# Four layers on one core: sums of denominators by matmul, scores moved, a bias multiplied as a row

## The chip, the cores and the metric

The kernel runs on one core of a Trainium2 chip. The metric is the device time of one execution in microseconds (us). Before the change it was 3402.58 us, the median of three runs (3399.19 to 3405.2).

## The reference

The input x has two images of 512 channels and 1024 pixels (32 by 32), all in float32. Four layers follow each other: layer 0 is a deformable attention with a learned bias and an MLP, layers 1 to 3 are attentions over the pixels of each image. Layer 1 has eight heads, layers 2 and 3 have one. The parts that the change touches are these:

```python
# layer 1: the projection and its bias; v carries the bias qkv_b[1024:]
out = jnp.einsum('oc,bcl->bol', proj_w, hh) + proj_b[None, :, None]
# layer 2
attn = jax.nn.softmax(jnp.einsum('bci,bcj->bij', q, k) * scale, axis=-1)
out = jnp.einsum('bcj,bij->bci', v, attn)
x = x + jnp.einsum('bchw,oc->bohw', out, w_proj) + b_proj
# layer 3: 64 channels in q and k
q = jnp.einsum('dc,bcn->bdn', wq, f) + bq[:, None]
k = jnp.einsum('dc,bcn->bdn', wk, f) + bk[:, None]
v = jnp.einsum('dc,bcn->bdn', wv, f) + bv[:, None]
qk = jnp.einsum('bdi,bdj->bij', q, k)
attn = jax.nn.softmax(qk, axis=1)
o = jnp.einsum('bci,bij->bcj', v, attn)
return gamma * o.reshape(b, c, h, w) + x
```

Layer 3's softmax is over the first pixel index, the one that is summed over with v.

## The kernel before

Layer 0 fills the first 2450 us or so and is not touched. Layers 1 to 3 (and layer 0's MLP) are in the function `layers`, from line 1053 on. An order is written out by hand there: inside `in_order` every engine takes its instructions in the order in which the program issues them, so an instruction that waits holds up everything behind it on its engine.

Large products are done in blocks of two by two with seven products in place of eight (a Strassen-like scheme). The function `group` (line 1370) does one such product: it takes four PSUM banks x, y, v and z out of eight that rotate, and calls `add(out, l, r)` seven times; each call is a run of `nk` matmuls with left block number `l` and right block number `r`. Copies on ScalarE (ACT) and sums on VectorE (DVE), called p1, p5, u2 (line 1413) and u3 (line 1424), prepare what `evict` then writes. Some of the seven operands on each side are sums of blocks (on the left s4 at number 2, s1 at 4, s2 at 5; on the right t4 at 3, t1 at 4, t2 at 5), made by `left_sums` (lines 1356 to 1359) and `right_sums` (lines 1365 to 1368).

The sums, normalizations and divisions that are not part of a group are "chores". They stand in queues (`Track`), and `do_chores(us, budget)`, which `group` calls three times, moves a planner's clock on by `us` and issues chores from the queues, in the order of the list `tracks`, until their planned costs use up `budget`. A number in a queue is a wait in the planner's clock. `flush` issues all that is left. The planner's clock only decides the place in the program; it is not the time on the chip.

In layers 2 and 3 each image is handled in two halves of 512 pixels. For each half there is an object of the class `Weights`: u0 and u1 in layer 2; in layer 3, a0 and a1 for image 0, b0 and b1 for image 1. `grow` makes the scores and their exponentials, in four chunks p. Each chunk holds two blocks of 128 pixels by 512. Where `shares` is true (layer 3), the weights themselves are multiplied by the reciprocals (`normalize`, line 1853, 128 by 1024 each) before they are used; in layer 2 the result is (line 1888). The denominators come about like this:

```python
if c % 2 and self.shares or c == 1:
    self.acc.append(unit("acc"))
    self.add(self.acc[-1], p[c - 1], p[c])   # DVE, line 1813
...
self.track.extend((2.0, (0.1, self.total), 4.0, (0.4, self.divisor)))
if self.shares:
    self.track.append(5.0)
```

`total` (line 1834) multiplies the sums by ones, on four column tiles of 32, copies the result to SBUF and sends it over DMA into the layout 128 by 4 (`few`); `divisor` (lines 1844 to 1849) adds the four parts, inverts them, and sends them to DRAM (`d`) and from there to all partitions (`r`).

The value groups (`values`, called by `layer_values`) make v transposed, named vT, with products named pmv; vs are the left sums of them. `weighed` multiplies v by the weights, in two groups per half (products named pw), and adds the result to x. In layer 3 it then stores x. SyncE (SP) issues all these DMAs on one queue.

Layer 3 before went: scores of a0; second weighting of layer 2's image 1; value groups of image 0, with two `grow` of a1 after the first and two after the second; weighting of a0 with the projections of image 1 between its groups; scores of b0; weighting of a1; value groups of image 1 with the scores of b1 among them; weighting of b0; weighting of b1.

In layer 1, `projection_bias` (line 1702) multiplies the bias of v by the projection: sixteen products with one column each, into the bank pb. p_b is used in `add_projection`, in products named ppr.

Of the kernel before, what the change touches and what calls it, by code (L numbers as in the profile page):

```python
# [12 lines left out]
F32 = mybir.dt.float32  # L13
# [6 lines left out]
P = 128  # L20
# [60 lines left out]
def kernel(ctx: ExitStack, tc: tile.TileContext, a: dict, out: bass.AP):  # L81
# [971 lines left out]
    def layers(f, fold_d, t2_b, o2_b):  # L1053
# [330 lines left out]
        def group(name, nk, n, stationary, moving, evict, slack, plain=False):  # L1384

            third = nk * n / 256

            x, y, v, z = [bank(name)[:, :n] for _ in range(4)]

            def add(out, l, r, start=True):  # L1390
                for k in range(nk):
                    nc.tensor.matmul(  # L1392
                        out,
                        stationary(l, k),
                        moving(r, k),
                        start=start and k == 0,
                        stop=k == nk - 1,
                        skip_group_check=not start,
                    )

            if plain:
                for out, (l, r) in ((x, (0, 0)), (y, (6, 0)), (v, (0, 6)), (z, (6, 6))):
                    add(out, l, r)
                    add(out, 1 if l == 0 else 3, 1 if r == 0 else 2, False)
                evict((x, None), (v, None), (y, None), (z, None))
                return
            later, put_off[:] = list(put_off), []
            add(x, 0, 0)
            p1 = temp("p1", n)
            nc.scalar.copy(p1, x)  # L1410
            add(y, 5, 5)
            u2 = temp("u2", n)
            nc.vector.tensor_tensor(u2, y, p1, ALU.add)  # L1413
            add(v, 4, 4)
            p5 = temp("p5", n)
            nc.scalar.copy(p5, v)
            at_once(later)
            do_chores(third, slack)
            add(z, 3, 3)
            add(x, 1, 1, False)  # L1420
            do_chores(third, slack)
            add(y, 6, 6, False)
            u3 = temp("u3", n)
            nc.vector.tensor_tensor(u3, y, p1, ALU.add)
            add(v, 2, 2, False)
            evict((x, None), (v, u2), (z, u3), (p5, u3))
            do_chores(third, slack)
# [78 lines left out]

        def values(seven_w, seven_h, s, vt):

            vq = vt.rearrange("p (k m n) -> p k m n", k=2, m=2)

            def evict(c11, c12, c21, c22):
                put(vq[:, 0, 0], c11)
                put(vq[:, 0, 1], c21)
                put(vq[:, 1, 1], c22)
                put(vq[:, 1, 0], c12)

            group(
                "pmv", 2, QUARTER,
                lambda i, k: seven_h[i][:, k, s * P : (s + 1) * P], lambda i, k: seven_w[i][:, k, :], evict, 1.1,
            )  # L1520
# [178 lines left out]
        p_b = keep.tile([P, CC], F32, name="p_b")  # L1699

        def projection_bias():
            pb = bank("pb")
            for m in range(CC):
                accumulate(
                    pb[:, m : m + 1],
                    [(proj1[k // 2][:, k % 2, m * P : (m + 1) * P], vb[:, 0, k : k + 1]) for k in range(CC)],
                )
            nc.vector.tensor_tensor(p_b, pb[:, :CC], col("proj_b", 0, CC), ALU.add)

# [7 lines left out]
        to_w = track()  # L1717
        to_w.append((0.3, projection_bias))
        w_p = weights_p()
        in_time(to_w, 0.5, left_sums(*w_p))  # L1720
        qs, ks = heads(seven_h)
        vt = every_value(seven_v, seven_h)
        flush(to_w, to_o)
        add_projection(xs[0], seven_left(*w_p), seven_o)
# [48 lines left out]

        def layer_values(seven_w, seven_h):

# [7 lines left out]
            def steps():  # L1783
                for s in range(4):
                    vt.append(unit("vT"))
                    values(seven_w, seven_h, s, vt[s])
                    unformed.append(s)
                    if s == 2:
                        sv.extend(unit("vs") for _ in range(3))
                    while sv and unformed:  # L1790
                        in_time(t_s, 0.45, left_sums(*parts(unformed.pop(0))))
                    yield
# [3 lines left out]
        class Weights:  # L1796

            def __init__(self, score, order, at, shares):
                self.score, self.order, self.at, self.shares = score, order, at, shares
                self.p, self.acc, self.spare, self.track = [], [], None, track()  # L1800

# [13 lines left out]
            def grown(self, c):  # L1815
                p = self.p
                if c % 2 and self.shares or c == 1:
                    self.acc.append(unit("acc"))
                    self.add(self.acc[-1], p[c - 1], p[c])
                elif c > 1 and not self.shares:  # L1820
                    self.add(self.acc[0], self.acc[0], p[c])
                if not self.shares:
                    for i in ((), (0, 1), (2,), (3,))[c]:
                        self.form(i)
# [3 lines left out]
            def total(self):  # L1828
                den, row = bank("den"), temp("row", HALF)
                n = 2 * len(self.acc)  # L1830
                self.few = small.tile([P, 4, HALF // P], F32, name="few2")
                for i in range(n):
                    acc = self.acc[i // 2].rearrange(self.order, k=2, q=2)
                    nc.tensor.matmul(den[32 * i : 32 * i + 32], ones[:, :32], acc[:, i % 2], start=True, stop=True)
                nc.scalar.copy(row[: 32 * n], den[: 32 * n])
# [5 lines left out]
            def divisor(self):  # L1841
                few = self.few[:, 0]
                for i in range(1, 2 * len(self.acc)):
                    nc.vector.tensor_add(few, few, self.few[:, i])
# [3 lines left out]
                nc.sync.dma_start(out=d.rearrange("(q n) -> q n", q=P), in_=few)  # L1848
                nc.sync.dma_start(out=self.r, in_=d.partition_broadcast(P))

            def normalize(self, c):
# [15 lines left out]
            def finish(self):  # L1867
                self.track.extend((2.0, (0.1, self.total), 4.0, (0.4, self.divisor)))
                if self.shares:
                    self.track.append(5.0)  # L1870
                    for c in range(4):
                        self.track.append((1.2, lambda c=c: self.normalize(c)))
                        self.form(c)

        def weighed(name, x, qb, seven_sv, w, bias, done=None):

            n = slice(qb * HALF, (qb + 1) * HALF)
            for g in range(2):

                def evict(c11, c12, c21, c22):  # L1880
# [15 lines left out]

                group(name, 4, QUARTER, lambda i, s: seven_sv(i, s)[:, g * P : (g + 1) * P], w.seven, evict, 2.6)
                yield
# [24 lines left out]
        for b in range(B):  # L1923
# [21 lines left out]
            if b == 0:  # L1945
                flush(to_h)
                to_h = track()
                seven_h = normed(to_h, norm, h2s[1], "h2")
                flush(u0.track, to_v)
                drain(weighed("pw2", xs[0], 0, value2, u0, o2_b))  # L1950
                flush(u1.track)
                drain(weighed("pw2", xs[0], 1, value2, u1, o2_b))
# [37 lines left out]

        def scores3(qb, both):

# [3 lines left out]
            def score(c):  # L1996
                p = unit("p3")
                for part, (l, r) in enumerate(((qk, kq), (kq, qk))):
# [31 lines left out]

        flush(u0.track, to_v)
        seven_x, to_x = pixels3(xs[0])
# [8 lines left out]
        for c in range(4):  # L2041
            a0.grow(c)
        flush(u1.track)
        drain(weighed("pw2", xs[1], 1, value2, u1, o2_b))
        flush(to_x)
        value3, value_steps, to_v = layer_values(seven_v3, seven_x)
        for c in range(2):
            advance(value_steps)
            a1.grow(2 * c)
            a1.grow(2 * c + 1)  # L2050
        drain(value_steps)
        flush(a0.track, to_v)
        steps = weighed("pw3", xs[0], 0, value3, a0, gb3, store(0))
# [3 lines left out]
        drain(steps)  # L2057
        b0, b1 = [scores3(qb, both) for qb in range(2)]
        for c in range(4):
            b0.grow(c)  # L2060
        flush(a1.track)
        drain(weighed("pw3", xs[0], 1, value3, a1, gb3, store(0)))
        flush(to_x)
        value3, value_steps, to_v = layer_values(seven_v3, seven_x)
        for c in range(2):
            advance(value_steps)
            b1.grow(2 * c)
            b1.grow(2 * c + 1)
        drain(value_steps)
        flush(b0.track, to_v)  # L2070
        steps = weighed("pw3", xs[1], 0, value3, b0, gb3, store(1))
        advance(steps)
        checks = guard()
        drain(steps)
        flush(b1.track)
        advance(checks)
        steps = weighed("pw3", xs[1], 1, value3, b1, gb3, store(1))
        advance(steps)
# [101 lines left out]
```

## The time and profile before

| What | us |
|---|---|
| median of three runs | 3402.58 |
| the profiled execution | 3400.25 |
| its span, first to last instruction | 3398.4 |
| PE busy in the span | 3351.9 |
| PE busy from 3350 to 3398 us (48 us) | 34.57 |
| four den products in layer 3 (eight records) | 1.00 |
| one normalize step on DVE (128 by 1024) | 1.22 |
| r<-d, from issue to landing, median from 3150 us on | 4.2 |
| few<-row, the same | 2.0 |
| out<-x, the same | 2.1 |

PE is TensorE's matmuls, PEld its weight loads, DVE VectorE, ACT ScalarE, SP SyncE's DMA queue. A float32 matmul leaves two records in the trace, so "x8" are four matmuls. The clock that the profile gives for PE is the share of full speed that was granted.

### The profile page before, as it was taken

How to read it: one execution, taken by the hardware profiler on the slowest of the kernel's cores; microseconds unless marked ns; L12 is line 12 of the kernel's file. 1: busy time of each engine (PE TensorE's matmuls, PEld its weight loads, DVE VectorE, ACT ScalarE, POOL GpSimd, SP SyncE). 2: the span in 40 equal slices, each digit the busy share in tenths (PEclk: the TensorE clock that was granted, in tenths of full speed). 3: DMA queues.
4: the chain of work that ended last, by engine and by line, in shares of the span. 5: the costliest groups of instructions: out<-in, count | busy, mean ns of one | idle time of the engine just before them, and what ended most of it. 6: DMA issues, size and time to landing. Idle time of an engine off the chain costs nothing.

```text
span 3398.4 us, 61331 instructions
## 1 busy us (share of the span) xinstructions
PE 3351.9 (99%) x24853; PEld 1615.5 (48%) x24853; DVE 2662.6 (78%) x3461; ACT 1803.4 (53%) x2764; POOL 464.0 (14%) x563
## 2 busy tenths in 40 slices
PE   9999999999999999999999999999999999999998
PEld 4333332333333333333333338999953533678676
DVE  6999999999997899999998954455456465756565
ACT  4866867867866667867867641112136245212221
POOL 0222222222221122222222210000000000000000
PEclk9999999999999999999999999999999999999999
DMA  5676676676775576676776641000100010000110
GB/s 167 149 151 139 141 153 143 139 153 138 148 149 118 110 150 138 149 148 137 150 147 142 141 124 57 14 11 11 51 0 14 26 35 14 7 7 5 28 38 30
DMA packets 146707, 320.31 MB, mean 94 GB/s; under 512 B 31088, under 2 KB 76784, under 8 KB 145648
## 3 DMA queue, kind: packets, MB, share of 16 engines
q0 software_dynamic: 56880, 199.79, 30.9%
q1 hardware_dynamic: 88240, 111.80, 10.9%
q8 instruction: 198, 3.24, 0.4%
q10 hardware_dynamic: 1296, 4.72, 0.4%
q14 instruction: 93, 0.76, 0.1%
HBM read 71.46 MB, written 10.83 MB: 24 GB/s over the span
## 4 chain that ended last, share of the span: by engine, by line
PE 77%; DVE 16%; issue 4%; ACT 2%; DMA 1%; ACTq 0%; POOL 0%; DVEq 0%; SPq 0%; POOLq 0%
PE z L543 35%; DVE wa L526 6%; PE pma L136 5%; PE pw L1392 5%; PE pmb L136 4%; DVE h L557 4%; PE pmv L1392 4%; PE score L1568 3%; PE pv L1580 3%; PE pm L1392 3%; PE score L1392 3%; DVE h L526 2%; PE pmp L136 2%; PE pp L629 2%; PE ppr L1392 1%
## 5 line engine op out<-in xcount | busy, mean ns | idle before, releaser
L543 PE MATMUL z<-wa,cpb_w 128*32 128x512 f32 x11904 | 1779.1, 593 | 6.7 <-DVE simbias L490 3.4
L552 ACT ACTIVATE h<-z,b2h 128x1024 f32<-128x1024 f32 x1024 | 1134.2, 1114 | 529.6 <-PE z L543 506.2
L543 PE MATMUL z<-h,cpb_w 128*32 128x512 f32 x4480 | 986.3, 593 | 3.3 <-ACT h L552 2.2
L543 PEld LDWEIGHTS z<-wa,cpb_w 128*32 128x32 f32 x11904 | 492.9, 110 | 883.6 <-issue 804.6
L526 DVE CUSTOM_DVE_ANT_1 wa<-tab,tab 128x1024 f32<-128x1024 f32 x744 | 878.2, 1216 | 34.0 <-PE z L543 33.9
L557 DVE SCALAR_TENSOR_TENSOR h<-h,turn,h 128x1024 f32<-128x1024 f32 x512 | 653.3, 1276 | 8.8 <-ACT h L552 8.6
L543 PEld LDWEIGHTS z<-h,cpb_w 128*32 128x32 f32 x4480 | 256.2, 110 | 335.0 <-issue 291.8
L832 POOL DMA_DIRECT2D h<-h x255 | 227.9, 894 | 1055.0 <-DVE h L557 711.4
L526 DVE CUSTOM_DVE_ANT_1 h<-tab,tab 128x1024 f32<-128x1024 f32 x280 | 332.9, 1216 | 10.5 <-PE z L543 10.4
L1214 ACT COPY p<-pma 128x128 f32<-128x128 f32 x70 | 18.6, 266 | 305.6 <-PE pma L136 305.6
L1569 ACT ACTIVATE p<-score 128x512 f32<-128x512 f32 x256 | 130.0, 626 | 81.2 <-PE score L1568 80.4
L1206 DVE TENSOR_TENSOR upper<-pma,p 128x256 f32<-128x256 f32 x70 | 29.5, 421 | 163.6 <-ACT p L1214 163.5
L825 POOL DMA_DIRECT2D h<-h x126 | 110.9, 880 | 322.4 <-DMA h<-h 319.0
L829 POOL DMA_DIRECT2D h<-h x126 | 119.0, 944 | 155.2 <-DMA h<-h 148.8
L1601 DVE TENSOR_TENSOR acc<-acc,p 128x1024 f32<-128x1024 f32 x96 | 111.1, 1217 | 20.7 <-ACT p L1569 20.6
L1568 PE MATMUL score<-q,k 64*128 64x512 f32 x512 | 120.7, 604 | 1.1 <-DVE gm L1088 1.1
L1580 PE MATMUL pv<-p,vT 128*64 128x512 f32 x512 | 116.5, 598 | 0.0
L1392 PE MATMUL pw<-p,vT 128*128 128x256 f32 x384 | 91.5, 385 | 6.9 <-DVE p L1853 6.9
L513 ACT ACTIVATE tab<-tab,pc 128x512 f32<-128x512 f32 x126 | 96.2, 763 | 0.0
L1392 PE MATMUL pmv<-wa,hc 128*128 128x256 f32 x384 | 89.7, 380 | 5.2 <-DVE u L1413 5.2
L347 ACT ACTIVATE products<-qpad,pc 128x64 f32<-128x64 f32 x252 | 85.5, 407 | 0.0
L1392 PEld LDWEIGHTS pw<-p,vT 128*128 128x128 f32 x384 | 72.4, 191 | 24.2 <-DVE p L1853 8.4
(432 smaller groups left out, 3680.2 us busy)
## 6 DMA issues: line engine op xcount, KB each, us to landing
h<-h POOLq DMA_DIRECT2D x255, 512.0 KB, 5.0
h<-h POOLq DMA_DIRECT2D x252, 256.0 KB, 4.7
tab<-slog_d SPq DMA_DIRECT2D x128, 256.0 KB, 4.6
h<-h SPq DMA_DIRECT2D x126, 256.0 KB, 2.3
r<-d SPq DMA_DIRECT2D x24, 256.0 KB, 3.5
xt<-in_xt SPq DMA_DIRECT2D x8, 512.0 KB, 7.6
wa<-in_mlp_w SPq DMA_DIRECT2D x4, 1024.0 KB, 7.9
wb<-in_mlp_w SPq DMA_DIRECT2D x16, 256.0 KB, 5.6
```

The source lines that it names most:

```text
L136: nc.tensor.matmul(pm, w, m, start=(k == 0), stop=(k == len(pairs) - 1))
L526: nc.vector._custom_dve(TENSOR_ADD_SAT, out=h1.rearrange("p (y x) -> p y x", x=W), in0=tx[:, quad, point, :].unsqueeze(1).to_broadcast([P, ...
L543: nc.tensor.matmul(z[point * 32 : point * 32 + 32, n], cpb_w2[:, lo : lo + 32], h1s[point][:, n], start=True, stop=True,)
L552: nc.scalar.activation(h2, z, AF.Relu, bias=b2h[:, part : part + 1])
L557: nc.vector.scalar_tensor_tensor(h2, h2, turn[:, part // 2 : part // 2 + 1], parts.pop(part + 1), ALU.mult, ALU.add)
L829: nc.gpsimd.dma_start(out=joins[i - 3][1:P:2], in_=joins.pop(i - 2)[1:P:2], accum_op=ALU.add)
L832: nc.gpsimd.dma_start(out=joins[i - 1], in_=other, accum_op=ALU.add)
L1392: nc.tensor.matmul(out, stationary(l, k), moving(r, k), start=start and k == 0, stop=k == nk - 1, skip_group_check=not start,)
L1568: nc.tensor.matmul(sc, ks[m][r, s * P : (s + 1) * P], qs[m][r, n], start=True, stop=True)
L1569: nc.scalar.activation(p[:, part], sc, AF.Exp, scale=64 ** -0.5)
L1580: nc.tensor.matmul(pv[half][part * 64 : part * 64 + 64], vt[s % 4][:, lo : lo + 64], lps[s, half][:, part, :], start=(s == 0), stop=(s == 7),)
L1601: nc.vector.tensor_add(acc[half], acc[half], ps[s, half])
```

## The change

- `group` with more than two chunks (`nk` > 2: the weightings of layers 2 and 3) calls `add(z, 3, 3)` second, right after `add(x, 0, 0)`, not fourth.
- `projection_bias` is split. `bias_row` takes the bias as the stationary operand, 32 columns wide by repetition, and the projection as the moving one, in four products on four column tiles; a copy and four small DMAs bring the row into 128 by 4 by 4. The four parts are added on DVE later.
- In layer 3 the denominators are products of ones with all four p, accumulated in PSUM; the sums acc on DVE go away.
- `total` and `divisor` of layer 3 stand in a queue of their own, `chain`, at the head of the list of queues; the planner's waits around them are 6.5, not 4.0 and 5.0. For layer 2 the first is 6.5 as well, in its old queue.
- a1's scores are grown ahead of the first two value groups, not after them. The value groups of layer 3 may do more chores in each third (1.7, not 1.1).
- b1's scores are made between and after the two groups of the weighting of a1, a weighting and more earlier; they lie in unused columns of the weights tile w_3.
- The last group of all evicts straight into x, in quarters of 256 columns.

```diff
@@ group
             nc.scalar.copy(p1, x)
+            if nk > 2:
+                add(z, 3, 3)
             add(y, 5, 5)
...
             do_chores(third, slack)
-            add(z, 3, 3)
+            if nk == 2:
+                add(z, 3, 3)
             add(x, 1, 1, False)
@@ layer 1
+        def bias_row():
+            pb, row = bank("pb"), temp("row", HALF)
+            for k in range(CC):
+                nc.tensor.matmul(
+                    pb[32 * k : 32 * k + 32],
+                    vb[:, 0, k : k + 1].to_broadcast([P, 32]),
+                    proj1[k // 2][:, k % 2, :].rearrange("p (m q) -> p q m", m=CC),
+                    start=True,
+                    stop=True,
+                )
+            nc.scalar.copy(row, pb)
+            with nc.allow_non_contiguous_dma("2048 numbers"):
+                for k in range(CC):
+                    nc.sync.dma_start(
+                        out=p_few[:, k], in_=row[32 * k : 32 * k + 1].rearrange("o (q m) -> o q m", m=CC)
+                    )
+
         def projection_bias():
-            pb = bank("pb")
-            for m in range(CC):
-                accumulate(
-                    pb[:, m : m + 1],
-                    [(proj1[k // 2][:, k % 2, m * P : (m + 1) * P], vb[:, 0, k : k + 1]) for k in range(CC)],
-                )
-            nc.vector.tensor_tensor(p_b, pb[:, :CC], col("proj_b", 0, CC), ALU.add)
+            nc.vector.tensor_tensor(p_b, p_few[:, 0], col("proj_b", 0, CC), ALU.add)
+            for k in range(1, CC):
+                nc.vector.tensor_add(p_b, p_b, p_few[:, k])
...
-        to_w.append((0.3, projection_bias))
+        to_w.append((0.3, bias_row))
+        to_b = track()
+        to_b.extend((15.0, (0.5, projection_bias)))
@@ Weights
-                if c % 2 and self.shares or c == 1:
-                    self.acc.append(unit("acc"))
-                    self.add(self.acc[-1], p[c - 1], p[c])
...
                 den, row = bank("den"), temp("row", HALF)
-                n = 2 * len(self.acc)
+                some = [p.rearrange(self.order, k=2, q=2) for p in (self.p if self.shares else self.acc)]
+                n = self.n = min(4, 2 * len(some))
...
+                for i in range(2 * len(some)):
+                    j = i % n
+                    nc.tensor.matmul(
+                        den[32 * j : 32 * j + 32],
+                        ones[:, :32],
+                        some[i // 2][:, i % 2],
+                        start=i < n,
+                        stop=i + n >= 2 * len(some),
+                    )
...
                 nc.sync.dma_start(out=self.r, in_=d.partition_broadcast(P))
+                if self.shares:
+                    self.track.ready = clock[0] + 6.5
+                    for c in range(4):
+                        self.track.append((1.2, lambda c=c: self.normalize(c)))
+                        self.form(c)
...
-                self.track.extend((2.0, (0.1, self.total), 4.0, (0.4, self.divisor)))
-                if self.shares:
-                    self.track.append(5.0)
...
+                (self.chain if self.shares else self.track).extend((2.0, (0.1, self.total), 6.5, (0.4, self.divisor)))
@@ weighed
+                def evict_last(c11, c12, c21, c22):
+                    for (base, more), i, q in ((c11, 0, 0), (c21, 1, 0), (c22, 1, 1), (c12, 0, 1)):
+                        m, at = g + 2 * i, qb * HALF + q * QUARTER
+                        dst = x[:, m, at : at + QUARTER]
+                        if more is not None:
+                            nc.vector.tensor_add(dst, dst, more)
+                        nc.vector.scalar_tensor_tensor(dst, base, bias[:, m : m + 1], dst, ALU.add, ALU.add)
+                        if q:
+                            done(m, n)
@@ scores3
-                p = unit("p3")
+                p = unit("p3") if places is None else places[:, c * HW : (c + 1) * HW]
@@ layer 3
-        value3, value_steps, to_v = layer_values(seven_v3, seven_x)
+        value3, value_steps, to_v = layer_values(seven_v3, seven_x, 1.7)
         for c in range(2):
-            advance(value_steps)
             a1.grow(2 * c)
             a1.grow(2 * c + 1)
+            advance(value_steps)
...
-        b0, b1 = [scores3(qb, both) for qb in range(2)]
+        spare = HALF + CC * C + 6 * QUARTER
+        b0, b1 = [scores3(qb, both, places) for qb, places in ((0, None), (1, w_3[:, spare : spare + CC * HW]))]
...
-        drain(weighed("pw3", xs[0], 1, value3, a1, gb3, store(0)))
-        flush(to_x)
-        value3, value_steps, to_v = layer_values(seven_v3, seven_x)
-        for c in range(2):
-            advance(value_steps)
+        for c, _ in enumerate(weighed("pw3", xs[0], 1, value3, a1, gb3, store(0))):
             b1.grow(2 * c)
             b1.grow(2 * c + 1)
+        flush(to_x)
+        value3, value_steps, to_v = layer_values(seven_v3, seven_x, 1.7)
...
-        steps = weighed("pw3", xs[1], 1, value3, b1, gb3, store(1))
+        steps = weighed("pw3", xs[1], 1, value3, b1, gb3, store(1), True)
```

## The prediction

> **What bounds the kernel now.** I read the page first, then TensorE's waits, then the timeline and the granted clock around the longest of them. Nothing before 2640 us changes in the order of any engine's work, so the question is what the last 760 us hold.
>
> ```profile
> PE 3351.9 (99%) x24853; PEld 1615.5 (48%) x24853; DVE 2662.6 (78%) x3461; ACT 1803.4 (53%) x2764; POOL 464.0 (14%) x563
> ```
>
> PE is busy 99% of the span, so a gain must come out of PE's own work, out of its few waits, or out of the end. The waits of PE from 2640 us on (engine, line, whom for, us in total, times, longest):
>
> ```profile
> PE pw L1392 <- DVE p L1853: 6.9, 3, 3.1
> PE pmv L1392 <- DVE u L1413: 5.2, 3, 3.7
> PE pw L1392 <- DVE vs L1357: 3.5, 4, 0.9
> PE score L1568 <- DVE gm L1088: 1.1, 1, 1.1
> PE score L1392 <- DVE u L1413: 0.7, 1, 0.7
> ```
>
> Only 17.4 us. But two of them cost more than they last. The timeline of PE, then the busy time and granted clock of stretches behind the two (PEclk is the number before the last two):
>
> ```profile
> 3212.41 1.13 PE L1392 MATMUL pmv<-wa,hc 128*128 128x256 f32 x4 [3.71 <-DVE u L1413]
> ...
> 3333.63 2.43 PE L1392 MATMUL pw<-pt,vs 128*128 128x256 f32 x10 [0.88 <-DVE vs L1357]
> ...
> 3359.76 0.70 PE L1392 MATMUL pw<-p,vT 128*128 128x256 f32 x2 [3.09 <-DVE p L1853]
> 3362.61 1.22 PE L1392 MATMUL pw<-p,vT 128*128 128x256 f32 x2 [2.15 <-DVE p L1853]
> 3365.45 1.22 PE L1392 MATMUL pw<-p,vT 128*128 128x256 f32 x2 [1.63 <-DVE p L1853]
> 3366.47 5.65 PE L1392 MATMUL pw<-pt,vs 128*128 128x256 f32 x16
> ```
>
> ```profile
> 3214.00:3216.00 2.00, 2.00 (x5) 0.84 (x5) 1.93 (x6) 0.00 (x0) 0.00 (x0) 0.50 0.00 0
> ...
> 3368.00:3370.00 2.00, 2.00 (x6) 1.55 (x6) 0.28 (x2) 0.00 (x0) 0.00 (x0) 0.50 0.00 0
> ```
>
> The reader is to see that after each pause the matmuls run at half the clock: sixteen records that take 3.62 us elsewhere took 5.65. Who keeps DVE from serving PE stands in DVE's timeline:
>
> ```profile
> 3202.00 1.22 DVE L1853 TENSOR_TENSOR p<-p,r 128x1024 f32<-128x1024 f32 x1 [5.21 <-DMA r<-d]
> ...
> 3352.66 1.23 DVE L1853 TENSOR_TENSOR p<-p,r 128x1024 f32<-128x1024 f32 x1 [4.51 <-DMA r<-d]
> ```
>
> DVE takes its instructions in order, and waits for the broadcast of the reciprocals with evictions queued behind it. Last, two pieces of the chain of waits that price PE's own work (start, us, what):
>
> ```profile
> 2648.84 3.47 PE pb L136 x32
> ...
> 3187.66 1.00 PE den L1834 x8
> ```
>
> [...] Here one-column pb records last 250 ns, their weight loads 192 ns. [...]matmuls on different column tiles overlap; four den products (eight records of about 605 ns) take 1.00 us together. [...]no strided moving operand is in the part of the trace I looked at, so its price is open.
>
> **The change, part by part.**
>
> *A. Last weighting (weights b1).* Before, b1 is scored between the value groups; den runs at 3339.5, r lands at 3352.6, and each of the four normalize steps with its sums takes about 2.9 us of DVE (1.22 and four of 0.42), so the fourth chunk is ready at 3365.4 where PE wanted it at 3357.4. That group runs from 3356.08 to 3378.95, 22.87 us; the next, of the same 56 records, takes 12.2 (3379.07 to 3391.28). Excess: 10.7 us, of which 6.9 are waits and 3.8 clock. After, b1's scores stand inside the weighting of a1, den in the first value group, and its normalize steps inside the two groups of b0. From den to b1's use lie over three value groups (6.05 each) and two weighting groups (12.2 each), 43 us. The chain wants 0.6 (row), 2.6 (four issues at 0.65), 2.0 (landing), 0.6, 1.6 (d), 4.2 (r) and 11.7 (four steps): 23 us. The planner adds waits of its own, yet some 5 to 20 us stay over. −10.7. What is late next there: nothing; the vs sums of value group four were needed earlier.
>
> *B. Wait of 3.71 us in image 0's value groups.* Before, a0's first normalize stands ahead of u3 of the last pw2 group and waits 5.21 us for r, so evictions slip, then two more normalize steps go ahead of the value groups' u. The matmuls from 3212.41 to 3217.90 take 5.5 us where their records at full clock take 3.65: 1.85 on top, 5.55 in all. After, the divisor is set 6.5 units behind the sums and normalize another 6.5 behind it, one unit being about a microsecond (a third of a weighting group counts 4 and lasts 4.1), against 5.6 to 5.8 us measured from divisor to r. The new order has the first normalize behind the eviction of the last pw2 group, with no DMA wait. Laid out by hand from the end of that group's matmuls: its eviction takes DVE to 3.4, normalize and sums to 6.3, u2, second normalize and sums to 9.7, half of a third (1.2) to 10.9, u3 to 11.3. PE does four scores (1.92), a value group (to 8.0), four scores (to 9.9); the next value group wants its y bank at 10.8, which is free at 11.3. So about 0.6 us of wait stay[...]. −4.95; bounds −5.5 and 0 (a wait of the old size).
>
> *C. The four vs waits.* With four chunks, add(z,3,3) now comes second. Its operands are a plain block of vT and a sum of weights formed long before; it gives DVE 1.73 us more ahead of the first vs product, and each wait was 0.87. All four go: −3.5. z's bank is wanted earlier, but eight banks rotate and its last reader is a group or four scores back.
>
> *D. Value bias as a row.* 16 products of one column (3.47 us) become four of 32 rows by 512 columns on four column tiles. At den's price 1.0[...]. I take 1.5: −2.0 (bounds −2.5 and +0.5). The ACT copy (0.58), four small DMAs on SP's queue (2.6 us of issue, ahead of a division's few), and four small adds on DVE lie beside heads and value groups; p_b is wanted by ppr 60 us later. Nothing on the path; up to 1 us if SP's d and r behind them slip.
>
> *E. Denominators from the weights.* Eight adds of 1.22 us leave DVE (9.8 us, not on the path as such), and four weightings get four more den products each: 4 × 1.0 = +4.0, fully on PE. Bounds +3.0 and +6 (if accumulating on a tile just used keeps them from overlapping).
>
> *F. End.* Before, the last x ends 2.1 us after the last matmul (c 0.44, x 0.67, x 0.74). After, u3 and seven 256-wide operations (0.42 each, 0.34 to 0.46 apart) start at the same point, 1.5 us before the last matmul ends, and end about 1.7 behind it: −0.4. Stores land in 2.1 us as before.
>
> *G. Value groups with slack 1.7, scores moved ahead, layer 2's later divisor.* DVE's load in image 0's value groups: 4 × 2.1 of evictions, 11.7 of normalize, 7.2 of vs sums, 27 us against PE's 24.2 + 3.8 + 2.0 = 30. It fits, less tightly than before without the adds. 0.
>
> Sum: −10.7 −4.95 −3.5 −2.0 +4.0 −0.4 = −17.5. The profiled execution took 3400.25 (span 3398.4 and 1.9 around it), 2.3 below the median of 3402.58. That gives 3382.7 from the one and 3385.1 from the other; I take 3384.
>
> **Rivals.**
> 1. DVE is late again in the value groups (27 of 30 us leaves little): waits [...]bring the half clock, at B's old price of 5.5 per image: 3384 + 5.5 to 11, about 3392. For it: u3 stands behind up to 4 us of queued sums. Against it: the layout above gives 0.6, and image 1 has no scores there any more.
> 2. D and E cost their upper bounds, +2.5 and +2: 3388.5.
> 3. Slower: the broadcast r, on SP's one queue with 256 KB stores, lands later than the planner's 6.5 units, and each weighting stalls as b1's did (10.7). To end above 3409 it takes 25 us back, so three of four weightings: 3384 + 32 = 3416. It decides where divisor to r passes about 9 us instead of 5.8. Against it: in SP's new order stores stand between the sums and the broadcast of b0 alone.
> 4. The change doesn't do what it says, b1's normalize steps staying late because the weights in w_3's spare columns make scores wait for readers of w_3: A is lost, 3395. The last such readers are long done.
>
> **How the numbers follow.** Main case 0.78, its own range 3379 to 3389. Rival 1 0.09, rival 2 0.07, rival 3 0.03, rival 4 0.03. The low end is every bound on the good side (D −2.5, E +3, B −5.5, and one microsecond at the end): about −20.5 to −23, 3378. The high end takes in rival 1: 3393. Differences under 0.2% (6.8 us) can't be told from none here. Faster is the main case, rivals 1 and 2 nearly whole, and half of 4: 0.93; same 0.04; slower 0.03.
>
> **What would show it.** Right: no wait of pw for the normalize line, no clock below 1 behind 3150 us, the last weighting's two groups alike at about 12.2 us, no wait for vs, den rows of about 2 us for x16, pb of 1 to 2 us, one pmv wait of some 0.6 in image 0. Wrong: DVE waiting for r with u3 behind it, a pmv wait over 3 us, or den rows well above 2 us.

## The result, and the profile after

| | before | after |
|---|---|---|
| median of six runs (lowest to highest), us | 3402.41 (3399.19 to 3405.2) | 3380.89 (3380.24 to 3382.41) |
| profiled execution, us | 3400.25 | 3381.55 |
| its span, us | 3398.4 | 3379.8 |

The ratio after to before is 0.9939, with a 95% interval of 0.9929 to 0.9949. The change took off 21.5 us by the medians and 18.6 us between the two profiled spans. The work ahead of 2644 us, where nothing changes, ran 0.66 us longer in the profiled execution of after (the first pm behind the last pv starts at 2644.16, before at 2643.50), so behind it 19.3 us went. The terms below are measured against that. The profiled execution of before was one of its faster ones (3400.25 us against a median of 3402.41); part D of the account below shows what the slower ones most likely have on top.

The first part of the page after (busy us, share of the span, instructions of each engine), and TensorE's waits from 2640 us on (line waited for, us in total, times, longest):

```profile
PE 3348.8 (99%) x24861; PEld 1611.8 (48%) x24861; DVE 2654.9 (79%) x3458; ACT 1804.6 (53%) x2764; POOL 464.7 (14%) x563
```

```profile
PE score L1571 <- DVE gm L1088: 1.1, 1, 1.1
PE score L1392 <- DVE u L1415: 0.7, 1, 0.7
PE pmv L1392 <- DVE u L1415: 0.3, 1, 0.3
```

Of 17.4 us of waits 2.1 are left. The waits for the normalize line, for vs and the 3.71 us are gone; the two for scores were there before, and the 0.3 us is what is left of two short waits in layer 2's value groups. PE's busy time fell by only 3.1 us although the half clock is gone as well, because the longer den products give some of it back.

The timeline of TensorE through the last weighting of after, and the busy time and granted clock (third from the end) of the stretch that ran at half clock before:

```profile
3347.73 1.89 PE L1392 MATMUL pw<-wa,vT 128*128 128x256 f32 x8
...
3358.09 1.89 PE L1392 MATMUL pw<-wa,vs 128*128 128x256 f32 x8
...
3360.03 1.99 PE L1392 MATMUL pw<-wa,vT 128*128 128x256 f32 x8
...
3370.49 1.89 PE L1392 MATMUL pw<-wa,vs 128*128 128x256 f32 x8
```

```profile
3368.00:3370.00 2.00, 2.00 (x11) 1.77 (x10) 0.00 (x0) 0.00 (x0) 0.00 (x0) 1.00 0.05 12
```

The two groups of that weighting now take 12.25 and 12.35 us from first to last matmul, at full clock: the first lost 10.6 of its 22.9 us, and the weighting as a whole 10.7 (35.35 to 24.65).

The chain of waits of after (start, us, what) prices the pieces of PE's own work that the change touched:

```profile
2649.51 2.26 PE pb L1709 x7
...
2991.16 12.09 PE pw L1392 x56
3003.25 0.98 PE den L1855 x4
3004.23 36.46 PE pw L1392 x168
...
3183.45 1.85 PE den L1855 x16
```

The reader is to see three things. The bias row costs 2.26 us, against 3.47 for the sixteen single columns. Eight den products (sixteen records) cost 1.85 us, against 1.00 for four. And the weighting of layer 2's image 0 runs from 2991.16 without a pause: with its den it takes 49.53 us to 3040.69. Before, the timeline has for the same records, and for the first ones behind them:

```profile
2992.92 1.89 PE L1392 MATMUL pw<-p,vT 128*128 128x256 f32 x8
...
3043.59 1.88 PE L1392 MATMUL pmt<-hc,wa 128*128 128x512 f32 x4
```

That is 50.67 us, with one wait of about 0.9 for vs in them, so that wait cost 1.14.

Last, DVE's timeline at the end of after:

```profile
3370.69 0.42 DVE L1427 TENSOR_TENSOR u<-pw,p 128x256 f32<-128x256 f32 x1 [4.68 <-PE pw L1392]
3371.04 0.47 DVE L1916 SCALAR_TENSOR_TENSOR x<-pw,gb,x 128x256 f32<-128x256 f32 x1
...
3373.72 0.48 DVE L1916 SCALAR_TENSOR_TENSOR x<-pw,gb,x 128x256 f32<-128x256 f32 x1
```

The last matmul ends at 3372.38, DVE at 3374.20. From the last matmul to the end of the span there are 7.4 us, against 7.0 before: the new end is not shorter.

### The profile page after: what moved, and what is told of

Read it like the earlier page. It is cut to its first block, busy times and chain, and to the rows that moved or that the text cites. A ratio compares the mean times of both kernels' runs of the same rounds, so it can differ in the third digit from the quotient of the medians.

```text
span 3379.8 us, 61349 instructions
## 1 busy us (share of the span) xinstructions
PE 3348.8 (99%) x24861; PEld 1611.8 (48%) x24861; DVE 2654.9 (79%) x3458; ACT 1804.6 (53%) x2764; POOL 464.7 (14%) x563
## 4 chain that ended last, share of the span: by engine, by line
PE 79%; DVE 15%; issue 4%; ACT 2%; DMA 0%; POOL 0%; DVEq 0%; SPq 0%; ACTq 0%; POOLq 0%
PE z L543 35%; DVE wa L526 6%; PE pw L1392 6%; PE pma L136 5%; PE pmb L136 4%; DVE h L557 4%; PE pmv L1392 4%; PE score L1571 3%; PE pv L1583 3%; PE pm L1392 3%; PE score L1392 3%; DVE h L526 2%; PE pmp L136 2%; PE pp L629 2%; PE pmt L1392 1%
## 5 line engine op out<-in xcount | busy, mean ns | idle before, releaser
L1214 ACT COPY p<-pma 128x128 f32<-128x128 f32 x70 | 18.6, 266 | 305.5 <-PE pma L136 305.5
L1571 PEld LDWEIGHTS score<-q,k 64*128 64x128 f32 x512 | 47.3, 186 | 70.3 <-issue 54.9
L1392 PEld LDWEIGHTS pmv<-wa,hc 128*128 128x128 f32 x384 | 72.6, 190 | 14.2 <-issue 2.8
```

The source lines that it names most:

```text
L1392: nc.tensor.matmul(out, stationary(l, k), moving(r, k), start=start and k == 0, stop=k == nk - 1, skip_group_check=not start,)
L1571: nc.tensor.matmul(sc, ks[m][r, s * P : (s + 1) * P], qs[m][r, n], start=True, stop=True)
```

## The experiments

Eight kernels were run. Each was timed against the kernel before on the same chip, whose medians there were 3402.54 us (e1 to e4) and 3403.07 us (e5 to e8). All compute the whole output.

The prediction had the right size for its largest step, A. The question was whether its reason holds. Theory 1 is the prediction's: the stall in the last weighting goes because b1's scores stand a weighting earlier, inside that of a1. Theory 2: b1's scores were early enough before; what came late was what DVE owes to them, the sums acc and the total, which stood behind other chores in b1's queue. The queue of its own at the head of the list, or taking the sums off DVE, cures that wherever the scores are.

### e1: the change with b1's scores back between the value groups

```diff
-        for c, _ in enumerate(weighed("pw3", xs[0], 1, value3, a1, gb3, store(0))):
-            b1.grow(2 * c)
-            b1.grow(2 * c + 1)
+        drain(weighed("pw3", xs[0], 1, value3, a1, gb3, store(0)))
         flush(to_x)
         value3, value_steps, to_v = layer_values(seven_v3, seven_x, 1.7)
+        for c in range(2):
+            b1.grow(2 * c)
+            b1.grow(2 * c + 1)
+            advance(value_steps)
         drain(value_steps)
...
-        b0, b1 = [scores3(qb, both, places) for qb, places in ((0, None), (1, w_3[:, spare : spare + CC * HW]))]
+        b0, b1 = [scores3(qb, both) for qb in range(2)]
```

> The changed kernel, but b1's scores are made ahead of image 1's first two value groups (as a1's are for image 0) and lie in the arena; everything else stays. Theory 1 (the prediction's step A: the early place of the scores is what removes the last stall): a good part of the stall comes back, the first group of the last weighting lasts 17 to 23 us and the median is 3386 to 3391. Theory 2 (the queue of their own is what brings the sums, the inversion and the normalize steps forward; the place of the scores matters little): that group lasts 12.2 us and the median is 3381 as with the change.

Measured: 3382.57 us (3381.55 to 3382.85), ratio 0.9944 (0.9928 to 0.9961), which can't be told from the change's own. The last den in its timeline of PE:

```profile
3308.92 1.92 PE L1855 MATMUL den<-p,ones 128*32 128x512 f32 x16
```

It stands 40 us ahead of the last weighting (3348.87), where the change has 46 (3301.74 to 3347.73). No wait of pw appears. With the queue and the products in place, the early place of the scores is not needed.

### e2: the kernel before with b1's scores early, alone

```diff
-        b0, b1 = [scores3(qb, both) for qb in range(2)]
+        spare = HALF + CC * C + 6 * QUARTER
+        b0, b1 = [scores3(qb, both, places) for qb, places in ((0, None), (1, w_3[:, spare : spare + CC * HW]))]
...
-        drain(weighed("pw3", xs[0], 1, value3, a1, gb3, store(0)))
-        flush(to_x)
-        value3, value_steps, to_v = layer_values(seven_v3, seven_x)
-        for c in range(2):
-            advance(value_steps)
+        for c, _ in enumerate(weighed("pw3", xs[0], 1, value3, a1, gb3, store(0))):
             b1.grow(2 * c)
             b1.grow(2 * c + 1)
+        flush(to_x)
+        value3, value_steps, to_v = layer_values(seven_v3, seven_x)
```

> The kernel before with this alone: b1's scores inside the weighting of a1, in the spare columns of w_3. Theory 1: the last stall goes, -10.7, 3392. Theory 2: b1's sums and inversion still stand behind the chores of b0 and the vs sums in the list of queues, so den stays just ahead of the last weighting and nothing is gained: 3402, last group 22 to 23 us.

Measured: 3402.71 us (3399.74 to 3405.05), ratio 1.0001 (0.9993 to 1.001). Nothing is gained. TensorE's timeline, b1's den and the waits behind it:

```profile
3342.26 1.06 PE L1834 MATMUL den<-acc,ones 128*32 128x512 f32 x8
...
3362.24 1.22 PE L1392 MATMUL pw<-wa,vT 128*128 128x256 f32 x2 [2.74 <-DVE wa L1853]
3365.08 1.22 PE L1392 MATMUL pw<-wa,vT 128*128 128x256 f32 x2 [1.63 <-DVE wa L1853]
3367.93 1.22 PE L1392 MATMUL pw<-wa,vT 128*128 128x256 f32 x2 [1.63 <-DVE wa L1853]
```

And DVE's timeline, the sums over b1's weights among b0's normalize steps, and the sums for vs behind them:

```profile
3296.89 1.21 DVE L1813 TENSOR_TENSOR acc<-wa 128x1024 f32<-128x1024 f32 x1
3310.56 1.21 DVE L1853 TENSOR_TENSOR p<-p,r 128x1024 f32<-128x1024 f32 x1
...
3323.03 1.22 DVE L1853 TENSOR_TENSOR p<-p,r 128x1024 f32<-128x1024 f32 x1
3327.49 1.22 DVE L1813 TENSOR_TENSOR acc<-wa 128x1024 f32<-128x1024 f32 x1
3328.96 0.41 DVE L1356 TENSOR_TENSOR vs<-vT 128x256 f32<-128x256 f32 x1
...
3336.78 0.42 DVE L1359 TENSOR_TENSOR vT<-vT 128x256 f32<-128x256 f32 x1
```

b1's last scores end at 3308.2, 9 us earlier than before by the same view. But the second sum comes at 3327.49, behind all four normalize steps of b0. Then the sixteen sums for vs follow (3328.96 to 3337.20), and only then total: the den at 3342.26 is 16.6 us ahead of the last weighting (3358.90), the same as before (3339.44 to 3356.08). The early scores only wait longer. Theory 1 falls.

### e3: the kernel before with the queue of its own, alone

The sums stay on DVE, and move into the queue too. The planner's waits are 6.5, as in the change.

```diff
-self.p, self.acc, self.spare, self.track = [], [], None, track()
+self.p, self.acc, self.spare, self.chain, self.track = [], [], None, track(True), track()
...
-                self.track.append((1.2, lambda: nc.vector.tensor_add(acc, one, other)))
+                (self.chain if self.shares else self.track).append((1.2, lambda: nc.vector.tensor_add(acc, one, other)))
...
-                self.track.extend((2.0, (0.1, self.total), 4.0, (0.4, self.divisor)))
-                if self.shares:
-                    self.track.append(5.0)
+                (self.chain if self.shares else self.track).extend((2.0, (0.1, self.total), 6.5, (0.4, self.divisor)))
```

> The kernel before with this alone: layer 3's sums (still on DVE), total and divisor in a queue at the head of the list, the planner's waits 6.5. Theory 1: the last stall stays as it was, 22.9 us; only part of the 3.7 us wait goes, 3398 or so. Theory 2: the last stall shrinks to one wait of about 2 us without the half clock (-8), and the 3.7 us wait to about 2.4 (-3): 3391.

Measured: 3393.6 us (3389.62 to 3395.48), ratio 0.9975 (0.9966 to 0.9984), 9 us faster (5.4 to 11.6 by the interval). TensorE's timeline:

```profile
3215.30 2.07 PE L1392 MATMUL pmv<-wa,hc 128*128 128x256 f32 x4 [2.16 <-DVE u L1413]
...
3327.72 1.06 PE L1834 MATMUL den<-acc,ones 128*32 128x512 f32 x8
...
3363.51 0.70 PE L1392 MATMUL pw<-p,vT 128*128 128x256 f32 x2 [1.87 <-DVE p L1858]
```

With the scores where they always were, b1's den comes 32.5 us ahead of the last weighting (3360.18), and three waits become one, with no half clock behind it (1.00 from 3363 to 3367). The first group takes 14.3 us (3360.18 to 3374.5) in place of 22.9: 8.6 of A's 10.7 come from the queue, with its order and its waits, alone. Which of the two does it was not tried apart.

### e6: the kernel before with denominators by products from the weights, alone

The old queue, its waits and the scores' place stay; only the sums leave DVE.

```diff
-                if c % 2 and self.shares or c == 1:
+                if not self.shares and c == 1:
...
-                n = 2 * len(self.acc)
+                some = [p.rearrange(self.order, k=2, q=2) for p in (self.p if self.shares else self.acc)]
+                n = self.n = min(4, 2 * len(some))
...
-                for i in range(n):
+                for i in range(2 * len(some)):
+                    j = i % n
```

> The kernel before with this alone: layer 3's denominators as products from the weights, in the old queues. If the sums on DVE are one of the things that hold den back behind other chores: den comes a value group earlier, the last stall shrinks to one wait of about 2 us at full clock (-8), the 3.7 us wait stays, PE has 3.4 more: 3398. If only the head of the queue helps: the stall stays, 3406.

Measured: 3397.23 us (3394.83 to 3404.46), ratio 0.9988 (0.9981 to 0.9995): a gain, 1.7 to 6.5 us by the interval. TensorE's timeline:

```profile
3324.96 1.92 PE L1835 MATMUL den<-p,ones 128*32 128x512 f32 x16
...
3363.34 0.70 PE L1392 MATMUL pw<-p,vT 128*128 128x256 f32 x2 [1.87 <-DVE p L1860]
```

The den stands 35 us ahead of the last weighting (3360.00), and the same single wait is left as in e3. So either edit cures most of that stall by itself, and here the products give some of it back: four times 0.85 us. In the value groups the old wait stays (3.38 us), but no half clock followed it in this execution; the last section shows the lines.

### e4: the change with the sums back on DVE, in the new queue

```diff
+                if self.shares and c % 2:
+                    self.acc.append(unit("acc"))
+                    one = self.acc[-1]
+                    self.chain.append((1.2, lambda: nc.vector.tensor_add(one, p[c - 1], p[c])))
...
-                some = [p.rearrange(self.order, k=2, q=2) for p in (self.p if self.shares else self.acc)]
+                some = [p.rearrange(self.order, k=2, q=2) for p in self.acc]
```

> The changed kernel with layer 3's denominators summed on DVE again, in the new queue. If the products from the weights only cost PE time (16 products, 0.85 us for each four by the trace of the changed kernel): -3.4, less some 2 us of new short waits: 3379 to 3380, den rows x8 of 1.0 us. If the sums on DVE are what made the stalls (rival): the waits of 3.7 us or the last stall come back, with the half clock: 3386 or more.

Measured: 3378.03 us (3377.56 to 3379.72), ratio 0.9933 (0.9916 to 0.9949), 2.9 us below the change's median, and no run of the one reaches those of the other. The two were timed at different times, and the intervals of their ratios overlap, but the traces agree: from the first pm behind the last pv to the end of the span there are 732.6 us here and 735.7 in the change. TensorE's waits from 2640 us on, whole:

```profile
PE score L1571 <- DVE gm L1088: 1.1, 1, 1.1
PE score L1392 <- DVE u L1415: 0.7, 1, 0.7
```

DVE has room for the sums, so with the queue in place the products from the weights bring nothing and cost PE about 3 us.

### e5: the kernel before with the vs order alone

```diff
             nc.scalar.copy(p1, x)
+            if nk > 2:
+                add(z, 3, 3)
             add(y, 5, 5)
...
-            add(z, 3, 3)
+            if nk == 2:
+                add(z, 3, 3)
```

> The kernel before with this alone: add(z, 3, 3) second in groups of more than two chunks. By the prediction's step C: the four waits for vs (0.87 each) go, -3.5. By the traces of before and after, where the stretches around two of them shrank by 1.3 each, the wait costs more than its row says: -5. Median 3397.5 to 3399. If another wait takes their place (rival): 3402.

Measured: 3397.39 us (3393.0 to 3399.03), ratio 0.9983 (0.9975 to 0.9991), so 3.1 to 8.5 us with a middle of 5.8. The row of vs is gone from its waits, and the weighting of layer 2's image 0 with its den takes 49.53 us (2996.56 to 3046.09), as in the change. Against the 50.67 of before that is 1.14 for one wait, not the 1.3 of the expectation, which mixed two views whose starts differ by 0.16. The other three stretches shrank by 1.14 as well, so four waits of 0.87 us are worth 4.6 in the traces, not 3.5; the interval of the times holds both.

### e7: the change with the old queue and the old waits

```diff
-                (self.chain if self.shares else self.track).extend((2.0, (0.1, self.total), 6.5, (0.4, self.divisor)))
+                self.track.extend((2.0, (0.1, self.total), 4.0, (0.4, self.divisor)))
...
-                    self.track.ready = clock[0] + 6.5
+                    self.track.ready = clock[0] + 5.0
```

> The changed kernel with total and divisor in the old queue and the planner's waits as before (4.0 and 5.0 for 6.5 and 6.5); sums by products, scores' places, slack and the order of the products stay. By the prediction's step B these waits are what removes the wait of 3.7 us: it comes back with the half clock, +5.5, 3386. Rival: with the sums gone and b1 scored early the old queue is enough, only a short pmv wait (1 to 2 us) comes: 3382 to 3383.

Measured: 3383.21 us (3382.57 to 3384.6), ratio 0.994 (0.9923 to 0.9956): 2.3 us above the change by the medians, and its span was 3.0 above. The intervals of the two ratios overlap, so the traces have to tell. DVE's timeline, then TensorE's, then the busy time and clock of stretches behind the wait:

```profile
3198.47 1.22 DVE L1885 TENSOR_TENSOR p<-p,r 128x1024 f32<-128x1024 f32 x1 [4.64 <-DMA r<-d]
```

```profile
3208.89 1.51 PE L1392 MATMUL pmv<-wa,hc 128*128 128x256 f32 x4 [2.24 <-DVE u L1415]
```

```profile
3208.00:3209.00 1.00, 0.11 (x1) 0.12 (x2) 1.00 (x4) 0.00 (x0) 0.00 (x0) 1.00 0.00 0
3210.00:3212.00 2.00, 2.00 (x5) 1.10 (x4) 1.93 (x5) 0.00 (x0) 0.00 (x0) 0.50 0.00 0
3213.00:3215.00 2.00, 2.00 (x11) 0.95 (x8) 1.93 (x6) 1.39 (x3) 0.00 (x0) 1.00 0.00 0
```

DVE's stall on the broadcast r is back at about its old length (4.64 us, 5.21 before), and with it a wait of PE, shorter than before (2.24 us, not 3.71), and a spell of half clock behind it (0.50 from 3210 to 3212). From the end of layer 2's weighting to the end of image 0's value groups there are 34.6 us here and 30.8 in the change. In the last weighting no wait came back: den is early (3310.78); e6 shows that taking the sums off DVE brings it forward in the old queue too. The queue and its waits are thus worth 2 to 4 us in the change, not B's 4.95.

### e8: the change, with what the runs had shown put together

The sums are on DVE (e4). The bias row reads proj in its plain order, and the ACT copy puts the row in the order wanted. In the last group the first quarter is evicted into x before the last products are done.

```diff
-                    proj1[k // 2][:, k % 2, :].rearrange("p (m q) -> p q m", m=CC),
+                    proj1[k // 2][:, k % 2, :],
...
-            nc.scalar.copy(row, pb)
+            nc.scalar.copy(row.rearrange("p (q m) -> p q m", m=CC), pb.rearrange("p (m q) -> p q m", m=CC))
...
+            if early is not None:
+                early(x, u2)
             add(y, 6, 6, False)
...
+                def early_last(c11, u2):
+                    dst = x[:, g, qb * HALF : qb * HALF + QUARTER]
+                    nc.vector.scalar_tensor_tensor(dst, c11, bias[:, g : g + 1], dst, ALU.add, ALU.add)
+                    dst = x[:, g, qb * HALF + QUARTER : (qb + 1) * HALF]
+                    nc.vector.tensor_add(dst, dst, u2)
```

> The changed kernel with three edits: the sums on DVE in the new queue (as in e4_sums_on_dve: -3), the value bias's products reading the projection without a step and ACT's copy permuting the row (pb rows 1.0 us for 2.3: -1.2), and in the last group the parts that need no late product added ahead of u3 (-0.7). Sum -4.9: 3376. If the DMA of the last stores sets the end whatever DVE does, 3377.

Measured: 3375.82 us (3374.96 to 3376.59), ratio 0.9918 (0.9902 to 0.9935): 5.1 us below the change and 27.2 below the kernel before. The instructions named pb, by tile (x instructions: shortest, median, longest ns), of the change and then of e8:

```profile
L1709 PE MATMUL pb<-proj,vb x8: 1047/1142/1337, 2649.4 to 2650.6; 128*32 128x512 f32 x8
```

```profile
L1711 PE MATMUL pb<-proj,vb x8: 592/604/616, 2649.1 to 2649.5; 128*32 128x512 f32 x8
```

By TensorE's timeline the four products took 1.06 us in place of 2.33, and the end after the last matmul 6.5 us in place of 7.4. With e4's part the three are worth 3.4 + 1.3 + 0.9 = 5.6 us by the traces, and 5.1 were measured.

## Why the prediction was right, and where it was not

The forecast, 3384, lay 3 us above the median of 3380.89, inside the range and inside the main case's own range (3379 to 3389). The signs of the terms were right but for F, which was of no weight. None of the rivals came: r landed in time, b1's normalize steps were early, no clock below 1 was granted to running matmuls behind 3150 us (1.00 in every stretch of 2 us up to 3374), and the one pmv wait left is 0.3 us. The nearness is in part luck: the sum missed about 2 us net, of terms that were off both ways, and it knew nothing of what the median of before most likely has on top of its profiled execution (D).

| step | predicted, us | measured in the profiles, us |
|---|---|---|
| A, last weighting | −10.7 | −10.7 |
| B, wait in image 0's value groups | −4.95 | −5.3 (the stretch shrank by 4.45, with a den in it that is 0.85 longer) |
| C, vs waits | −3.5 | −4.6 |
| D, bias row | −2.0 | −1.1 (from the first pm behind the last pv to the next den) |
| E, den products | +4.0 | +3.4 |
| F, end | −0.4 | +0.45 |
| layer 2's pmv waits | not named | −1.5 |
| sum | −17.5 | −19.3, and −19.3 from 2644 us on |

*A* is right in size and wrong in its reason. The step said that after the change "b1's scores stand inside the weighting of a1", and counted den's distance from there. The prediction had the chain's parts right, but took the scores' end as its start. The trace of before already showed that scores don't start it. b1's last scores ended near 3317.4, and DVE's timeline goes on like this:

```profile
3320.16 1.22 DVE L1853 TENSOR_TENSOR p<-p,r 128x1024 f32<-128x1024 f32 x1
...
3324.66 1.22 DVE L1813 TENSOR_TENSOR acc<-p,p 128x1024 f32<-128x1024 f32 x1
...
3334.78 1.21 DVE L1813 TENSOR_TENSOR acc<-p,p 128x1024 f32<-128x1024 f32 x1
```

The first sum over b1's weights stands behind the last normalize step of b0, the second behind the sixteen sums for vs as well, and den follows at 3339.44. e2 moves the scores alone and gains nothing; e1 takes them back and loses nothing that can be measured; e3 and e6 each bring den forward with the scores unmoved, and each leaves one wait of 1.87 us in place of three, which is 8.6 of the 10.7 us in both. That both together remove it wholly is seen in e1, which has both and the old place of the scores.

*B* is right in what it saw, DVE held up on r with evictions queued behind it, and e7 brings that stall back at 4.64 us. But the step put the whole 5.5 us on the queue and its waits. With both undone the wait is 2.24 us and the loss 2.3 by the medians, 3.8 by the stretch in the traces. In the kernel before, the queue and its waits alone leave a wait of 2.16 us (e3). So neither the queue nor the other edits do it alone. The rest must come from the other edits of the change, of which the sums off DVE alone is not the one (e6, on the old queue, keeps 3.38); whether it is a1's scores standing ahead of the groups or the larger slack was not tried apart. Its 0.6 us of remaining wait came out as next to nothing in image 0's groups.

*C* was mis-sized. The term was "four waits of 0.87". Each of the four stretches with one shrank by 1.14 us (50.67 to 49.53 in layer 2's image 0, and as much in its image 1, in a0 and in b0), and e5 gives 5.8 (3.1 to 8.5) for the four. The row counts only idle time between matmuls that the profile could tie to a releaser. What the other 0.27 us of each are is not shown.

*D* was mis-sized: 1.5 was taken for the four products, between den's price of 1.0 and an upper bound that was the author's estimate and that no trace showed, and 2.26 it was. e8 puts a price on the step here: with the step of 512 bytes a product's records took 1142 ns (median), without it 604. Why is not shown.

The step also missed something about the old form. In e2, TensorE's timeline at pb, then busy time and granted clock:

```profile
2648.97 4.22 PE L136 MATMUL pb<-vb,proj 128*128 128x1 f32 x32
2653.06 3.76 PE L1392 MATMUL pm<-h1t,wa 128*128 128x512 f32 x4
```

```profile
2650.00:2652.00 2.00, 2.00 (x20) 2.00 (x19) 0.00 (x0) 0.00 (x0) 0.00 (x0) 0.96 0.00 0
2654.00:2656.00 2.00, 2.00 (x4) 0.92 (x3) 1.93 (x4) 0.00 (x0) 0.00 (x0) 0.50 0.00 0
```

No wait stands there, yet the clock falls to 0.50 while the single columns run or just behind them, and four pm records take 3.76 us in place of 1.96. The profiled execution of before does not have it (1.00 from 2640 to 2700). From the first pm behind the last pv to the next den there are 12.35 us in that one and 15.7 in e2; e3 and e5 have 15.7 too, and e6 14.05. In the five traces with the bias row (after, e1, e4, e7, e8) there are 10.0 to 11.2, and in that of after the clock stays at 1 (1.00 from 2640 to 2700). So the row can save up to 4.5 us in an execution, not only 1.1. That this is why the medians lie 21.5 apart and the profiled spans 18.6 is likely and not shown, since no run took the row alone.

*E* was mis-sized by 0.15 for each weighting: the second eight records cost 0.85, not 1.0, so accumulating onto a column tile just used did not keep them from overlapping (records of some 600 ns each, eight of them in 0.85 us). e4 shows the term in the time: 2.9 us.

*F* took seven operations at 0.42 us, 0.34 to 0.46 apart. Those with three operands take 0.48 (first of them 0.47), they start 0.39 to 0.52 apart, and the last ends 1.8 us behind the last matmul, where 1.7 was said. Before it was 2.0, not 2.1: the last matmul ended at 3391.43, not at 3391.28. The span's end did not follow: from DVE's end to it were 5.0 us before (3393.40 to 3398.4) and 5.6 after (3374.20 to 3379.8).

*G* holds: DVE kept up. What was left out is a gain. Before, layer 2's value groups had two short pmv waits (0.25 at 2896.30, 1.27 at 2903.88); they are down to the 0.3 of the row shown above, and the stretch is 1.5 shorter. The second is 1.25 to 1.27 us in all five traces without the bias row and at most 0.30 in the five with it. e7 has it gone with the old waits of the planner, so they are not the cause; how the row or what comes with it does it is not shown.

## What to carry to other kernels

When a result comes late, follow its chain backwards on the engine that works in order, through every small step, before moving its first producer: here the scores were early enough, and sums and a total standing behind another consumer's normalize steps and the sums for vs held up the rest. A moved producer gains nothing until the slowest link behind it moves; giving that link a queue of its own, at the head, took no instruction more and was worth 9 us in e3. When a change holds two cures for one wait, undo them one at a time: the dearer one (eight products for four in each weighting) was not needed. And read the traces of several executions: the loss around the single columns (1.7 to 3.4 us) was in four of five, and not in the one that the prediction was made from.

## What was not expected of the hardware

- TensorE's clock fell to 0.50 after waits of 2.24 us (e7) and 2.16 us (e3, 0.50 from 3216 to 3218) and not after 1.87 us (the last weighting of e3 and of e6, 1.00 from 3363 to 3367). But the length of a wait did not decide it: after 3.71 us (before), 3.57 (e2) and 3.49 (e5) at the same place the second four pmv records took 1.73, 1.61 and 1.82 us, and in e6, after 3.38 us, 1.03 at a clock of 1.00, by TensorE's timeline and the clock behind the wait:

```profile
3214.23 1.13 PE L1392 MATMUL pmv<-wa,hc 128*128 128x256 f32 x4 [3.38 <-DVE u L1413]
```

```profile
3214.00:3216.00 2.00, 1.77 (x8) 1.44 (x8) 1.93 (x4) 0.00 (x0) 0.00 (x0) 1.00 0.00 0
3216.00:3218.00 2.00, 2.00 (x10) 0.69 (x8) 1.93 (x6) 0.68 (x2) 0.00 (x0) 1.00 0.00 0
```

  In e7 the clock granted in the four microseconds from 3209 on was 0.75, 0.50, 0.50 and 0.55, and 1.00 before and behind them: by an estimate from these, half clock for some 3.4 us (from about 3209.5 to 3212.9). The stretch of value groups was 3.8 us longer than in the change, about 1.6 more than the wait itself. What decides whether the clock falls is not shown by these runs.
- The clock also fell with no wait at all: in e2 to 0.50 (2654 to 2656), behind sixteen single-column products whose weight loads filled the time (PEld busy 2.00 of 2 us). In four of the five traces that have these products the stretch to the next den was 1.7 to 3.4 us longer than in the fifth (14.05 and 15.7 us against 12.35).
- The float32 moving operand with a step of 512 bytes cost 2.2 times as much here: 2.33 us for four products of 512 columns in the change (e8's kernel without the step: 1.06), by TensorE's timeline.
- Where the half clock is gone the times are also steadier: the six runs of after lie within 2.2 us, the 34 runs of before beside e5 to e8 within 9.1 us. That the clock's fall is what scatters them was not tried.
